# Perceiver block on one core: context loads placed between the transposes through DRAM, block-diagonal keys on ScalarE, the router's shares ahead of the softmax

## The chip, the core and the metric

The kernel runs on one core of a Trainium2 chip. The metric is the device time of one execution in microseconds (us). The kernel before was timed three times: 978.39 us median, 974.41 to 979.80. One execution was profiled; that one took 974.96 us, and its span, from the first to the last instruction in the trace, is 972.9 us. Engines in the profile: PE (TensorE matmuls), PEld (its weight loads), DVE (VectorE), ACT (ScalarE), POOL (GpSimd), SP (SyncE). ACTq, SPq and POOLq are the instruction queues of those engines where they issue DMAs.

## What is computed

There are 16 batches of 128 latent rows of 512 numbers, each with its own context of 2048 rows of 512, all float32. Per batch:

```python
x = x + softmax(LN(x) @ ctx.T) @ ctx          # cross attention, no scale, one head
h = LN(x)                                     # self attention, 16 heads of 32, causal
q, k, v = (h @ W_down) per head @ W_up        # half of q and k gets rotary positions
x = x + softmax(mask(q @ k.T / sqrt(32))) @ v @ Wc
h = LN(x)                                     # mixture of 8 experts of rank 64
gates = softmax over the top 2 of h[row 0] @ Wr.T
x = x + h + sum over the 2 of gate * (h @ A.T) @ B.T
```

Both experts are chosen for a whole batch by its first row.

## The kernel before, in words

The program is straight-line code for one core. A generator per batch and stage yields between small pieces of work, and `step(kind, batch, n)` runs the next n pieces. The order in which the pieces are issued is written out by hand: lines 616 to 668 for the start, the loop at line 671 for batches 0 to 13, lines 715 on for the last two. Matmuls, DMA issues and some others keep the order of the program on their engine; a scheduler may move the rest within an engine. Every engine then runs its own list strictly in order and waits on semaphores.

The stages of a batch, with the names that the profile shows:

- `score` (L250): normalizes x (`h_1`), turns it to `hT1`, multiplies it with the turned context `ctxT` in four parts v (`psc`, 32 matmul instructions each). ScalarE copies each to `sc` (L269), VectorE keeps a running maximum `mx`. Then the maximum over the context is spread over partitions (`tr_m`, `diag`, `spread`), added, and ScalarE takes the exponential (L297). A last piece adds up `sums` and `part` on VectorE.
- `attend` (L310): four parts of `av`, eight instructions each, and between the third and the last part `den`, the sum for the denominator, out of `part`. Then `x1` and its normalization `h_2`.
- `inner` (L332): `hT2`, then the projections `v`, `k` and `q` with folded weights. `rotated` (L360) applies the rotary positions: VectorE shuffles partners, GpSimd multiplies them (L376, `kP` and `qP`), VectorE multiplies and adds. `blocked` (L383) makes `kb`, k masked to one head of each pair, by four VectorE multiplies (L388). `compare` is `pss`, 16 instructions into four PSUM banks; `weigh` does the softmax of four heads at a time with VectorE and ScalarE (L415 to L429, 16 exps L424). Then `tr_p` transposes the probabilities on TensorE in four groups, ScalarE copies them out (`pT`, L167), and `y`, `o`, `x2` and `h_3` follow.
- `experts` (L563): `res = x2 + h_3` on GpSimd, `hT3`, `shares` (L472) and `route` (L487): `lg`, the logits, the two best, the indices, three gathers by indirect DMA on GpSimd's queue (`each` twice and `wb`), the copy `wa`, and the gate (L520 to L526). Then `mid`, `ffn`, the sum into `o` (L596) and its write to DRAM from GpSimd's queue (L597).

Batches overlap: while batch b is in `inner`, b+1 is in `attend`, b+2 in `score` and b-1 in `experts`. The pools p1, p2, p3, p4 hold one, two, three and four buffers of each name.

From batch 2 on (for hT1), from 1 to 14 (hT2) and from 0 to 13 (hT3), h is turned through DRAM: VectorE transposes blocks of 32x32 (`blocks`, L173), `send` (L142) writes them to a DRAM tile (`there`), and `fetch` (L150) reads them back in another order. Both are DMAs on SP's queue, and a fetch waits until its send has landed. In the loop the three transposes of a round are those of `3_{b-1}`, `2_{b+1}` and `1_{b+3}`.

The context goes through ScalarE's queue from the loop on: `load_ctx` and `load_turned` issue DMAs of 1 MB each, in ScalarE's program order, eight a batch. In the loop before, ctx 0, 1 and 2 of batch b+2 come between pieces of `inner` and `attend` (lines 683, 686, 690), and ctx 3 and the four ctxT of batch b+3 between the four `psc` of batch b+2 (lines 695 to 700), while `2_{b+1}` and then `1_{b+3}` are sent and fetched.

The few lines that place them, before:

```python
        step(inner, b + 1)
        send(f"2_{b + 1}")
        fetch(f"2_{b + 1}")
        step(experts, b - 1)
        for v in range(VC):
            step(score, b + 2)
            if v == 0:
                load_ctx(b + 2, [3])
            if b + 3 < B:
                load_turned(b + 3, [v])
```

Of the kernel before, what the change touches and what calls it, by code (L numbers as in the profile page):

```python
# [11 lines left out]
F32 = mybir.dt.float32  # L12
# [3 lines left out]
ALU = mybir.AluOpType  # L16
# [3 lines left out]
P = 128  # L20
# [48 lines left out]
def perceiver_block(ctx: ExitStack, tc: tile.TileContext, io: dict, out: bass.AP):  # L69
# [38 lines left out]
    def column(at):  # L108
        return cst[:, at : at + 1]
# [140 lines left out]
    def score(b):  # L250

        h = layernorm(xs[b], f"1_{b}", mix=b < 2)
        yield
        hT = p1.tile([P, 4, KC, QD], F32, tag="hT1", name=f"hT1_{b}")
        transposed(h, hT, f"1_{b}", b < 2)
        yield

        sc = p2.tile([P, VC, 4, S], F32, tag="sc", name=f"sc_{b}")
        mx = p1.tile([P, 4, S], F32, tag="mx", name=f"mx_{b}")
        for v, ct in enumerate(turned_cts.pop(b)):  # L260
            ps = bank(ps_sc, "sc", f"psc_{b}_{v}").rearrange("p (j t) -> p j t", j=4)
            for j in range(4):
                for c in range(KC):
                    matmul(
                        ps[:, j, :].rearrange("p (a i) -> p a i", a=4),
                        ct[:, c, j * P : (j + 1) * P], hT[:, :, c, :],
                        start=(c == 0), stop=(c == KC - 1),
                    )
            nc.scalar.copy(sc[:, v], ps)  # L269

            if v:
                nc.vector.tensor_tensor(mx, ps, mx if v > 1 else sc[:, 0], ALU.max)  # L272
            if v < VC - 1:
                yield

        def halved(t, op):
            nc.vector.tensor_tensor(t[:, :2], t[:, :2], t[:, 2:], op)
            nc.vector.tensor_tensor(t[:, 0], t[:, 0], t[:, 1], op)
            return t[:, 0]

        most = halved(mx, ALU.max)
        yield

        tr = bank(ps_tr, "tr", f"tr_m_{b}")
        transpose(tr[:, :S], most, ident)
        nm = p2.tile([P, 1], F32, tag="nm", name=f"nm_{b}")
        nc.vector.tensor_reduce(nm, tr[:, :S], AX.X, ALU.max, negate=True)
        diag = p1.tile([P, S], F32, tag="diag", name=f"diag_{b}")
        nc.vector.tensor_scalar(diag, ident, nm, None, ALU.mult)
        yield  # L290
        spread = bank(ps_tr, "tr", f"spread_{b}")
        matmul(spread[:, :S], ones, diag, start=True, stop=True)
        for v in range(VC):
            nc.vector.tensor_tensor(  # L294
                sc[:, v], sc[:, v], spread[:, None, :S].to_broadcast([P, 4, S]), ALU.add
            )
            nc.scalar.activation(sc[:, v], sc[:, v], AF.Exp)  # L297
        part = p2.tile([P, S], F32, tag="part", name=f"part_{b}")
        scores[b] = (sc, part)
        yield  # L300
        sums = p1.tile([P, 4, S], F32, tag="sums", name=f"sums_{b}")
        for v in range(1, VC):
            tc.keep_in_program_order(
                nc.vector.tensor_tensor(sums, sc[:, v], sums if v > 1 else sc[:, 0], ALU.add)
            )
        nc.vector.tensor_tensor(sums[:, :2], sums[:, :2], sums[:, 2:], ALU.add)
        nc.vector.tensor_tensor(part, sums[:, 0], sums[:, 1], ALU.add)
        yield

    def attend(b):  # L310

        sc, part = scores.pop(b)
        acc = bank(ps_acc, "acc", f"av_{b}")
        for v, ct in enumerate(cts.pop(b)):
            for j in range(4):
                matmul(
                    acc, sc[:, v, j, :], ct[:, j, :],
                    start=(v == 0 and j == 0), stop=(v == VC - 1 and j == 3),
                )
            if v == VC - 2:  # L320
                den = bank(ps_tr, "tr", f"den_{b}")
                matmul(den[:, :1], part, ones[:, :1], start=True, stop=True)
                rden = p2.tile([P, 1], F32, tag="rden", name=f"rden_{b}")
                nc.vector.reciprocal(rden, den[:, :1])
            if v < VC - 1:
                yield
        x1 = p2.tile([P, D], F32, tag="x1", name=f"x1_{b}")
        nc.vector.scalar_tensor_tensor(x1, acc, rden, xs.pop(b), ALU.mult, ALU.add)
        firsts[b] = (x1, layernorm(x1, f"2_{b}", mix=b in (0, B - 1)))
        yield  # L330

    def inner(b):  # L332
# [50 lines left out]
        def blocked():  # L383

            rotated("k", kT)
            for c in range(HC):
                kb = p4.tile([P, 2, S], F32, tag="kb", name=f"kb_{b}_{c}")
                nc.vector.tensor_tensor(  # L388
                    kb,
                    kT[:, c : c + 1, :].to_broadcast([P, 2, S]),  # L390
                    cst[:, C_BLK : C_BLK + 2, None].to_broadcast([P, 2, S]),
                    ALU.mult,
                )
                kbs.append(kb)

        def compare():

# [89 lines left out]
    def route(b, part):  # L487
# [29 lines left out]
            wa.rearrange("p c i r -> p i c r"), each.rearrange("p i (c r) -> p i c r", c=KC)  # L517
        )
        wa = wa.rearrange("p c i r -> p c (i r)")
        nm, ex, dn, gate = small(b, 1, "nm"), small(b, 1, "ex"), small(b, 1, "dn"), small(b, 1, "gate")  # L520
        nc.vector.tensor_scalar_mul(nm, top[:, 0:1], -1.0)
        nc.scalar.activation(ex, top[:, 1:2], AF.Exp, bias=nm)
# [6 lines left out]
    def early(b):  # L529
# [28 lines left out]
        part = shares(b, column_of(h, f"row_{b}"))  # L558
        yield
        route(b, part)  # L560
        yield

    def experts(b):  # L563

        x2, h = lasts.pop(b)
        res = p1.tile([P, D], F32, tag="res", name=f"res_{b}")
        if b < B - 2:
            nc.gpsimd.tensor_tensor(res, x2, h, ALU.add)
        else:
            nc.gpsimd.tensor_tensor(plain(res), plain(x2), mixed(h), ALU.add)  # L570
        hT = p1.tile([P, 4, KC, QD], F32, tag="hT3", name=f"hT3_{b}")
        transposed(h, hT, f"3_{b}", b >= B - 2)
        yield
        if b not in routes:
            part = shares(b, hT[:, 0, :, 0])
            yield
            route(b, part)
            yield
        wa, wb, gate = routes.pop(b)
        ps = bank(ps_acc, "acc", f"mid_{b}")  # L580
        for c in range(KC):
            matmul(
                ps[:, :S].rearrange("p (a i) -> p a i", a=4), wa[:, c, :], hT[:, :, c, :],
                start=(c == 0), stop=(c == KC - 1),
            )
        mid = p2.tile([P, S], F32, tag="mid", name=f"mid_{b}")
        nc.scalar.activation(mid, ps[:, :S], AF.Copy, scale=gate)
        yield
        o = p1.tile([P, D], F32, tag="o", name=f"out_{b}")

        n = D // 2 if b == B - 1 else D
        for at in range(0, D, n):
            cols = slice(at, at + n)
            ps = bank(ps_acc, "acc", f"ffn_{b}_{at}")
            matmul(ps[:, cols], mid, wb[:, cols], start=True, stop=True)
            nc.vector.tensor_tensor(o[:, cols], ps[:, cols], res[:, cols], ALU.add)  # L596
            (nc.sync if b == B - 1 else nc.gpsimd).dma_start(out[b][:, cols], o[:, cols])  # L597
        yield


# [66 lines left out]
    fold_turned(*ready)  # L667
    step(inner, 0)

    queue = nc.scalar  # L670
    for b in range(B - 2):
        if b + 3 < B:
# [2 lines left out]
        send(f"3_{b - 1}")  # L675
        fetch(f"3_{b - 1}")
        step(inner, b, 2)
        step(attend, b + 1)
        step(inner, b)
        step(score, b + 1)  # L680
        step(attend, b + 1)
        step(inner, b, 2)
        load_ctx(b + 2, [0])
        step(attend, b + 1)
        step(inner, b)
        load_ctx(b + 2, [1])
        step(experts, b - 1)
        step(attend, b + 1)
        step(inner, b)
        load_ctx(b + 2, [2])  # L690
        step(inner, b + 1)
        send(f"2_{b + 1}")
        fetch(f"2_{b + 1}")
        step(experts, b - 1)
        for v in range(VC):
            step(score, b + 2)
            if v == 0:
                load_ctx(b + 2, [3])
            if b + 3 < B:
                load_turned(b + 3, [v])  # L700
        step(inner, b)
        step(experts, b - 1)
        step(inner, b)
        step(experts, b - 1)
        step(inner, b)
        step(inner, b + 1)
        step(score, b + 2)
        step(score, b + 3, 2)
        send(f"1_{b + 3}")
        fetch(f"1_{b + 3}")  # L710
        step(inner, b)
        step(score, b + 2)

# [5 lines left out]
    step(inner, y, 2)  # L719
    step(attend, z)  # L720
    step(inner, y)
    step(score, z)
    step(attend, z)
    step(inner, y, 2)
    step(attend, z)
    step(inner, y)
    step(experts, y - 1)
    step(attend, z)
    step(inner, y)
    step(experts, y - 1)  # L730
# [10 lines left out]
    step(inner, z)  # L741
    step(experts, y)
    step(early, z)
    step(experts, y, 2)
    step(early, z)
    step(inner, z, 3)
    step(experts, y)
    step(inner, z)
    step(experts, y)
    step(experts, z, 3)  # L750


# [41 lines left out]
```

## Time and profile before

| | before |
|---|---|
| median of 3 runs | 978.39 us (974.41 to 979.80) |
| profiled execution | 974.96 us, span 972.9 us |
| PE busy | 863.3 us, 89% of the span |
| DVE, ACT, POOL busy | 511.7, 252.2, 169.6 us |
| DMA | 181.64 MB, 187 GB/s over the span |
| mean granted TensorE clock | 0.962 |
| loads of ctx and ctxT on ACTq | 56 and 52 DMAs of 1024 KB |
| sends and fetches on SPq | 42 and 42 of 256 KB |

How to read it. "X <- Y: total, times, longest" is a wait: instructions X stood idle, and the last thing they waited for was Y. A line of the chain of waits is start, length, what; it is the work that ended last, followed back. A line of the timeline is start, length, engine, source line, operation, out<-in, shapes, count, and in brackets the engine's idle time just before. L93 and L96 are the helpers that record every matmul and transpose, L101 the one that records DMA issues, so the tile's name tells the stage. A line of a table of stretches is from:to, length, busy time of PE, PEld, DVE, ACT and POOL with instruction counts, the granted clock, the busy share of the 16 DMA engines, and GB/s. Batch b's `pss` is the mark used for a period; in the trace those of batches 0, 1 and 14 start at 85.43, 137.77 and 891.45 us.

### The profile page before, as it was taken

What the parts mean: (1) busy time and instruction counts of PE and PEld (TensorE: products, weight loads), DVE (VectorE), ACT (ScalarE), POOL (GpSimd) and SP (SyncE); (2) the same over time, 40 slices, a digit from 0 to 9 for tenths busy, and PEclk for the clock granted to TensorE, in tenths of its full rate; (3) what the DMA queues carried; (4) which work ended last, traced back from release to release, by engine and by line L of the source; (5) the groups of instructions that cost most, each with busy time, mean ns of one, the idle gap of its engine ahead of it and who ended that gap; (6) DMA issues with size and microseconds to landing.
All of it is one profiled execution on the core that took longest, in us unless ns stands there. A gap on an engine that the chain in (4) does not pass through costs nothing.

```text
span 972.9 us, 14850 instructions
## 1 busy us (share of the span) xinstructions
PE 863.3 (89%) x5738; PEld 607.1 (62%) x5738; DVE 511.7 (53%) x1276; ACT 252.2 (26%) x787; POOL 169.6 (17%) x232
## 2 busy tenths in 40 slices
PE   7999998998979988899887989889799889999895
PEld 6846767565575755757555675655757557585653
DVE  1466374471835628275381744718356283837561
ACT  1232222231311322222222222313113222322340
POOL 1001012210122101212111121201221111121323
PEclk9999999998999999999899998999999999999987
DMA  9995819255282643808247182562826437240001
GB/s 362 347 407 198 311 44 355 99 213 222 81 313 84 253 181 149 306 23 344 100 162 281 31 348 98 189 244 82 311 85 259 174 152 292 85 166 22 22 18 58
DMA packets 57909, 181.64 MB, mean 187 GB/s; under 512 B 5504, under 2 KB 27392, under 8 KB 41456
## 3 DMA queue, kind: packets, MB, share of 16 engines
q10 hardware_dynamic: 15696, 113.32, 30.2%
q1 hardware_dynamic: 38064, 54.86, 15.6%
q0 software_dynamic: 4080, 12.53, 3.4%
q8 instruction: 45, 0.74, 0.3%
q14 instruction: 24, 0.20, 0.1%
HBM read 165.48 MB, written 15.20 MB: 186 GB/s over the span
## 4 chain that ended last, share of the span: by engine, by line
PE 47%; DMA 22%; DVE 18%; POOL 7%; issue 4%; ACT 2%; ACTq 0%; SPq 0%; POOLq 0%; DVEq 0%
PE av L93 17%; DMA hT<-there 15%; DMA there<-blocks 7%; PE o L93 6%; PE v L93 6%; PE psc L93 5%; DVE sc L294 3%; PE ffn L93 2%; DVE kb L388 2%; POOL rs L128 2%; DVE st L121 2%; POOL kP L376 2%; POOL qP L376 2%; PE y L93 2%; PE pss_sc L93 2%
## 5 line engine op out<-in xcount | busy, mean ns | idle before, releaser
L93 PE MATMUL psc<-hT,ctxT 128*128 128x128 f32 x2048 | 236.0, 278 | 1.4 <-ACT hT L167 1.4
L93 PEld LDWEIGHTS psc<-hT,ctxT 128*128 128x128 f32 x2048 | 233.3, 194 | 3.0 <-ACT hT L167 2.0
L93 PE MATMUL av<-ctx,sc 128*128 128x512 f32 x512 | 230.2, 598 | 0.0
L93 PEld LDWEIGHTS av<-ctx,sc 128*128 128x128 f32 x512 | 93.4, 190 | 104.3 <-issue 104.0
L424 ACT ACTIVATE att<-att,nmx 128x128 f32<-128x128 f32 x256 | 99.0, 388 | 196.0 <-DVE nmx L422 196.0
L125 POOL TENSOR_SCALAR rs<-mv 128x1 f32<-128x1 f32 x48 | 11.2, 233 | 461.3 <-DVE mv L123 445.9
L96 PE MATMUL tr_p<-ident,att 128*128 128x128 f32 x256 | 41.3, 306 | 46.7 <-ACT pT L167 46.7
L269 ACT COPY sc<-psc 128x512 f32<-128x512 f32 x64 | 37.5, 586 | 164.4 <-PE psc L93 164.4
L272 DVE TENSOR_TENSOR mx<-psc,mx 128x512 f32<-128x512 f32 x32 | 22.1, 691 | 91.9 <-ACT sc L269 91.9
L93 PE MATMUL v<-w_v,hT 128*32 128x512 f32 x512 | 61.1, 612 | 3.7 <-DMA hT<-there 2.8
L96 PEld LDWEIGHTS tr_p<-ident,att 128*128 128x128 f32 x256 | 33.0, 158 | 49.4 <-ACT pT L167 49.3
L297 ACT ACTIVATE sc<-sc 128x512 f32<-128x512 f32 x64 | 40.2, 630 | 90.9 <-DVE sc L294 90.4
L93 PE MATMUL o<-w_c,yT 128*128 128x512 f32 x128 | 60.9, 621 | 1.3 <-ACT yT L459 1.3
L93 PE MATMUL k<-hT,w_k 128*128 128x128 f32 x512 | 61.4, 279 | 0.7 <-ACT hT L167 0.7
L93 PEld LDWEIGHTS k<-hT,w_k 128*128 128x128 f32 x512 | 59.9, 196 | 1.8 <-ACT hT L167 0.9
L93 PE MATMUL q<-hT,w_q 128*128 128x128 f32 x512 | 59.8, 275 | 0.0
L93 PEld LDWEIGHTS q<-hT,w_q 128*128 128x128 f32 x512 | 58.5, 192 | 0.0
L596 DVE TENSOR_TENSOR out<-ffn,res 128x512 f32<-128x512 f32 (+1 forms) x17 | 11.2, 659 | 88.5 <-PE ffn L93 88.5
L167 ACT COPY pT<-tr_p 128x512 f32<-128x512 f32 x64 | 35.1, 592 | 68.8 <-DMA hT<-there 39.1
L424 ACT ACTIVATION_READ_ACCUMULATOR att<-att,nmx 128x1 f32 x256 | 47.7, 186 | 0.0
L294 DVE TENSOR_TENSOR sc<-sc,spread 128x512 f32<-128x512 f32 x64 | 42.6, 672 | 3.3 <-PE spread L93 3.3
L429 DVE TENSOR_TENSOR att<-att,rsm 128x512 f32<-128x512 f32 x64 | 43.6, 681 | 1.1
(127 smaller groups left out, 944.1 us busy)
## 6 DMA issues: line engine op xcount, KB each, us to landing
ctx<-in_ctx_dram ACTq DMA_DIRECT2D x56, 1024.0 KB
ctxT<-in_ctxT_dram ACTq DMA_DIRECT2D x52, 1024.0 KB
ctxT<-in_ctxT_dram SPq DMA_DIRECT2D x12, 1024.0 KB
there<-blocks SPq DMA_DIRECT2D x42, 256.0 KB
hT<-there SPq DMA_DIRECT2D x42, 256.0 KB
ctx<-in_ctx_dram SPq DMA_DIRECT2D x8, 1024.0 KB
x<-in_x_dram SPq DMA_DIRECT2D x16, 256.0 KB
out_dram<-out POOLq DMA_DIRECT2D x15, 256.0 KB, 2.9
```

Source lines behind the costliest of these rows:

```text
L93: tc.keep_in_program_order(nc.tensor.matmul(*args, **kwargs))
L96: tc.keep_in_program_order(nc.tensor.transpose(*args))
L121: nc.vector.bn_stats(stats, src)
L128: nc.gpsimd.tensor_tensor(rstd, rstd, mhalf[:n], ALU.pow)
L167: nc.scalar.copy(dst[:, :, first : first + 4, :].rearrange("p a n j -> p n a j"), tr.rearrange("p (n a j) -> p n a j", n=4, a=4),)
L269: nc.scalar.copy(sc[:, v], ps)
L272: nc.vector.tensor_tensor(mx, ps, mx if v > 1 else sc[:, 0], ALU.max)
L294: nc.vector.tensor_tensor(sc[:, v], sc[:, v], spread[:, None, :S].to_broadcast([P, 4, S]), ALU.add)
L297: nc.scalar.activation(sc[:, v], sc[:, v], AF.Exp)
L376: nc.gpsimd.tensor_tensor(partner, partner, cst[:, None, C_SIN : C_SIN + S].to_broadcast([P, HC, S]), ALU.mult)
L424: nc.scalar.activation(att[:, i, :], att[:, i, :], AF.Exp, bias=nmx[:, i : i + 1], scale=SCALE, accum_out=sm[:, i : i + 1],)
L429: nc.vector.tensor_tensor(att[:, hs, :], att[:, hs, :], rsm[:, hs, None].to_broadcast([P, 4, S]), ALU.mult)
```

## The change

- hT1 gets two buffers instead of one.
- `den` moves behind the last part of `av` for batches 1 to 14.
- `kb` is one tile made by two ScalarE activations (copy with a per-partition scale) instead of four tiles by four VectorE multiplies.
- `route` ends with the gathers; the gate's part is a function of its own, `gates`, issued in a later piece.
- `experts` adds `ffn` into `res` and writes `res` to DRAM; the tile `o` is gone.
- The loop is reordered: `experts` of b-1 takes its shares and `route` between pieces of `inner` and `attend`, that is ahead of the softmax; the sums of `score` come later; the four ctx loads of b+2 stand together behind the third `psc`, after the sends of `2_{b+1}` and `1_{b+3}`; ctxT 0 and 1 of b+3 come once `inner` of b+1 has issued its v, and ctxT 2 and 3 of b+2 at the start of the next round, behind the fetch of `3_{b-1}`.
- In the tail, `o` of batch 15 stands ahead of `mid` of batch 14.

```diff
-        hT = p1.tile([P, 4, KC, QD], F32, tag="hT1", name=f"hT1_{b}")
+        hT = p2.tile([P, 4, KC, QD], F32, tag="hT1", name=f"hT1_{b}")
...
-            if v == VC - 2:
+            if v == (VC - 1 if 0 < b < B - 1 else VC - 2):
                 den = bank(ps_tr, "tr", f"den_{b}")
...
-            for c in range(HC):
-                kb = p4.tile([P, 2, S], F32, tag="kb", name=f"kb_{b}_{c}")
-                nc.vector.tensor_tensor(
-                    kb,
-                    kT[:, c : c + 1, :].to_broadcast([P, 2, S]),
-                    cst[:, C_BLK : C_BLK + 2, None].to_broadcast([P, 2, S]),
-                    ALU.mult,
-                )
-                kbs.append(kb)
+            kb = p1.tile([P, HC, 2, S], F32, tag="kb", name=f"kb_{b}")
+            for half in range(2):
+                nc.scalar.activation(
+                    kb[:, :, half, :], kT, AF.Copy, scale=column(C_BLK + half)
+                )
+            kbs.extend(kb[:, c] for c in range(HC))
...
+        routes[b] = (wa, wb, top)
+
+    def gates(b):
+        wa, wb, top = routes[b]
         nm, ex, dn, gate = small(b, 1, "nm"), small(b, 1, "ex"), small(b, 1, "dn"), small(b, 1, "gate")
...
             route(b, part)
             yield
+            gates(b)
+            yield
...
-            nc.vector.tensor_tensor(o[:, cols], ps[:, cols], res[:, cols], ALU.add)
-            (nc.sync if b == B - 1 else nc.gpsimd).dma_start(out[b][:, cols], o[:, cols])
+            nc.vector.tensor_tensor(res[:, cols], ps[:, cols], res[:, cols], ALU.add)
+            (nc.sync if b == B - 1 else nc.gpsimd).dma_start(out[b][:, cols], res[:, cols])
...
         step(inner, b, 2)
+        if b:
+            load_turned(b + 2, [2, 3])
         step(attend, b + 1)
         step(inner, b)
+        step(experts, b - 1)
+        step(attend, b + 1)
+        step(experts, b - 1)
+        step(inner, b, 2)
         step(score, b + 1)
         step(attend, b + 1)
-        step(inner, b, 2)
-        load_ctx(b + 2, [0])
+        step(inner, b)
         step(attend, b + 1)
         step(inner, b)
-        load_ctx(b + 2, [1])
         step(experts, b - 1)
-        step(attend, b + 1)
-        step(inner, b)
-        load_ctx(b + 2, [2])
         step(inner, b + 1)
         send(f"2_{b + 1}")
         fetch(f"2_{b + 1}")
-        step(experts, b - 1)
-        for v in range(VC):
-            step(score, b + 2)
-            if v == 0:
-                load_ctx(b + 2, [3])
-            if b + 3 < B:
-                load_turned(b + 3, [v])
+        step(score, b + 3, 2)
+        send(f"1_{b + 3}")
+        step(score, b + 2, 3)
+        load_ctx(b + 2)
+        step(score, b + 2)
+        fetch(f"1_{b + 3}")
         step(inner, b)
...
         step(inner, b + 1)
+        if b + 3 < B:
+            load_turned(b + 3, [0, 1])
         step(score, b + 2)
-        step(score, b + 3, 2)
-        send(f"1_{b + 3}")
-        fetch(f"1_{b + 3}")
         step(inner, b)
         step(score, b + 2)
...
     step(early, z)
+    step(experts, y, 3)
+    step(early, z)
+    step(inner, z, 4)
     step(experts, y, 2)
-    step(early, z)
-    step(inner, z, 3)
-    step(experts, y)
-    step(inner, z)
-    step(experts, y)
     step(experts, z, 3)
```

## The prediction

> **What bounds the kernel now.** I read TensorE's waits first, then the chain of waits, then the timeline around the largest wait, and last a table of stretches.
>
> TensorE's waits (us in total, times, longest):
> ```profile
> PE tr_p L96 <- ACT pT L167: 46.7, 11, 5.0
> PE pss_sc L93 <- DVE qT L379: 22.9, 15, 1.6
> PE lg L93 <- DVE g_part L484: 13.1, 14, 1.0
> ```
> Three waits recur, the first in 11 batches, the others in nearly all; the rest are single ones. The first says that ScalarE's copy of pT came late. The chain of one period (start, us, what) says why:
> ```profile
> 507.49 2.23 DMA there<-blocks
> 509.81 15.47 DMA hT<-there
> 525.30 0.33 ACTq L101
> 525.73 0.59 ACT pT L167
> 526.37 1.11 PE tr_p L96 x4
> ```
> A transpose through DRAM is open for 17.7 us, of which 15.47 are its second half. Then ScalarE's queue issues a load (ACTq L101), and only then copies pT. The order of the built program names the link: the load of ctxT v=3 waits on the semaphore that hT2's fetch raises, because DMAs share a few semaphores in turn, and pT's copies stand behind it. The timeline shows the same instant:
> ```profile
> 519.19 0.59 ACT L269 COPY sc<-psc 128x512 f32<-128x512 f32 x1 [2.99 <-PE psc L93]
> 525.30 0.33 ACTq L101 DMA_DIRECT2D ctxT<-in_ctxT_dram  x1
> 525.73 1.07 ACT L167 COPY pT<-tr_p 128x512 f32<-128x512 f32 x2 [5.95 <-DMA hT<-there]
> 526.37 1.11 PE L96 MATMUL tr_p<-ident,att 128*128 128x128 f32 x4 [5.01 <-ACT pT L167]
> 527.28 1.93 PE L93 MATMUL ffn<-wb,mid 128*128 128x512 f32 x2
> ```
> ScalarE stands from 519.8 to 525.7, TensorE 5.01 us, and after it runs at half speed for a while: ffn takes 1.93, against 1.02 where nothing stalled (at 816.69). Why the fetch takes 15.47 is seen by its twin at 545.08, which has no loads beside it. In the stretches its bytes stand alone (DMA share, GB/s last):
> ```profile
> 546.00:548.00 2.00, 2.00 (x6) 0.76 (x4) 2.00 (x7) 0.00 (x0) 0.00 (x0) 1.00 0.43 131
> 548.00:550.00 2.00, 0.43 (x1) 0.00 (x0) 1.13 (x3) 0.00 (x0) 1.27 (x1) 1.00 0.00 0
> 512.00:518.00 6.00, 6.00 (x57) 6.00 (x56) 1.38 (x2) 1.17 (x2) 1.48 (x2) 1.00 1.02 413
> ```
> All its data moved before 548, under 3 us after issue; at 512 to 518 the same fetch shares full DMA engines with context loads.
>
> What a period costs, from the start of one batch's pss to the next (columns: length, PE busy, ..., clock, DMA):
> ```profile
> 490.72:550.05 59.33, 51.76 (x345) 36.50 (x346) 31.41 (x80) 15.09 (x48) 10.42 (x14) 0.97 0.49 187
> 838.95:891.45 52.50, 49.94 (x345) 35.82 (x346) 29.87 (x76) 15.13 (x48) 9.63 (x12) 1.00 0.33 116
> ```
> The second period is the last of the loop, with no further context to load: same matmuls, no pT wait, 52.50 us, clock 1.00. From batch 1's pss (137.77) to batch 14's (891.45) the 13 periods average 57.98. TensorE bounds it, with stalls of about 8 us a period.
>
> **The change, part by part.** t is time from a period's pss; durations are those of the rows above and of the timeline.
>
> *Loads.* ctxT 2 and 3 are issued behind the new kb on ScalarE (t about -1.6), ctx 0 to 3 behind the copy of psc 2 (t 24.1), ctxT 0 and 1 behind vv (t 36). In the built program none of them waits for a transpose still open: their semaphores belong to DMAs that landed over 5 us earlier. So ScalarE no longer stands before pT, and the 5.01 us with the slow matmuls go. The bounds of this term are nothing (a load still finds a wait of its own) and 5.01 plus the slow clock; I take the whole, because the period without the wait stands in the trace. What is late next: v needs hT2. den ends at t 12.8; behind it VectorE still has two multiplies, six small operations and 1/den, so x1 ends near 14.8; statistics, GpSimd's rstd (0.8), two normalizations and the block transpose bring blocks to 19.5; there lands 2.2 later, the clean fetch 2.9 after that, at 24.6. v starts at 31.6 (psc ends at 27.2, then tr_p, mid, tr_p, ffn and y, 4.4): 7 us to spare. hT1 follows by t 25.3, while the first load's data start near 25.5. Eight issues of 0.33 to 0.45 us stand on ScalarE beside psc and o, under 1.7 us together between two psc copies 3.6 apart: hidden. At the start SP issued five such loads from 1.18 to 4.05 us without standing, so four in a row should pass; if the cover were gone the delay would be that 1.7. The 6.3 MB of ctx and ctxT 0, 1 at the 404 GB/s seen at 26 to 36 us take 15.6 us, to t 41; hT3's fetch is issued at t 45. Context is first needed at t 46 (ctx) and t 62.8 (psc).
>
> *kb on ScalarE.* Four VectorE multiplies (1.37 us in the chain at 545.78) become two ScalarE operations of 128x512. No row has that operation; a plain copy of this size takes 0.59, an exp 0.63, and mid, with the same kind of scale on 128x128, 0.37: between 0.4 and 0.63 each. I take 0.6, the rows of its size, so 1.2 together, started when kT is ready (t -3.4) on an idle ScalarE: done at -2.1, ahead of pss. qT's chain (shuffle 0.7, GpSimd 1.27, add 0.69) starts 1.37 earlier and ends at av's end, so of the 1.62 wait about 0.1 is left. GpSimd's two products are then the end of it.
>
> *Shares and route.* g_share now runs right after qT, ahead of the softmax, and lg stands between av 1 and av 2. hT3 lands at t -2.2, g_share wants it at -0.1, lg at 5.4: the 0.94 wait goes. The softmax's sums move behind route's small operations, and den behind the last av. The VectorE walk, with the steps of batch 15's rows (922.36 on) and starting at its gap of 1.16: two adds and two reduces of 0.61 to 3.55, then two maxima, two adds and two reduces to 6.15 (ScalarE's exps run from 3.8, 1.55 a group of four), the first multiply to 6.75, lg's copy, a reciprocal, maxima for the third group (7.2), top, the second multiply to 7.95, the index, the first sum to 8.7, maxima for the fourth group (8.9; its exps end at 10.6), two more sums with blocks, row and rows between them to 10.75, the half sum to 11.1, two reciprocals, part at 11.6. den wants it at 12.64 (1.92 pss, 3.49 av, 0.25 lg, 6.98 two av). Zero cost, 1.0 spare; the bounds are that and the 2 us of rival 1. lg's own place costs TensorE the same 0.25 as before.
>
> *Others.* hT1 with two buffers and res instead of o remove or add waits that rows show as long over; g_ex is issued before psc, hidden behind 16 exps.
>
> Sum of a period: 52.50 - 1.62 - 0.94 + 0.1 = **50.05**, and the busy column of that period, 49.94, agrees. 13 x (57.98 - 50.05) = 103.1.
>
> *First period* (85.43 to 137.77, 52.34): it has a wait of 2.33 for hT2 (at 118.03) and 1.5 for qT: -3.8.
>
> *Tail* (891.45 to 972.90). For batch 15 den stays before the last av, but its part now comes at 11.7 while den's turn is 9.15: +2.6, bounds +1.5 to +6 (the upper with the last av's 3.5 us at half speed). h_2 loses its queue of g_ operations: -0.3. The o projection of batch 15 (953.45) stands ahead of mid_14, which waited for GpSimd's wa: yT can be copied at 950.2, so o starts 3.25 earlier, and GpSimd's rstd no longer stands behind the result's write (0.6): about -4.5 at the last add, where res_15 waits for res_14's write to land (2.9) and comes in just beside ffn. Together -2.2, bounds -4 to +2.
> Whether the 2.6 us cool the clock: after 2.33 idle v still took 3.64, full speed; after 2.48 and 0.68 idle k took 5.27 against 3.74. I take no cooling. The Trainium skill (TensorE: Matmul & The Clock Gate, Part 1) has the clock halved only after an idle window of about 3.4 us; by it this is safe too, by k's row the tail is 1.5 longer.
>
> Total: 972.9 - 103.1 - 3.8 - 2.2 = 863.8, plus the 2.06 around the span (974.96 - 972.9) = 865.9. The profiled execution lies 0.35% under the median 978.39; scaled by it: **869**.
>
> **Rivals.**
> 1. *A new wait per period.* The margin of den (1.0) is worked from steps of 0.1 to 0.7, and qT and av end within 0.2 of each other. If two of them cost 1 to 2 us a period: 13 to 26 more, 882 to 895. For: the walk is long. Against: every step has a row. 0.16.
> 2. *The result's write holds res.* res has one buffer, and GpSimd's res, ahead of the product for kP, waits until the last write has landed. Issue t 31.7, res wanted at 41.9. Rows have the write at 2.4 to 4.5; if it stretched to 15.5 beside the loads as the fetch did, res ends 3.4 us after kP's turn: 13 x 3.4 = 44, 913. Against: its rows are 2 KB, the fetch's 512 B. 0.05. The Trainium skill (DMA: Bandwidth & Descriptors, Queues, rings and completion order) has each DMA engine take turns between queues packet by packet; by that a write in a quarter of the packets should stretch to about 4 us, an estimate, and res stays free.
> 3. *Slower: hT3's fetch meets loads.* g_share stands ahead of the whole softmax. If ctx and ctxT 0, 1 run past t 45, that is under 6.3 MB / 19.5 us = 323 GB/s, the fetch takes 15.5, lands at 10.5, and the softmax starts 9.7 late: lg stalls 5.4, den 3.3, slow clock 1.5: period 60.2, 13 x 2.2 = 29 over before, less 6 elsewhere: 1001. Against: full engines show 391 to 423 GB/s everywhere. 0.05.
> 4. *It doesn't separate them*: the pT wait stays, only 2.5 a period go: 978 - 13 x 2.5 - 6 = 940. Against: the waits in the built program. 0.03.
>
> **Numbers.** Forecast 0.71, rivals 0.16, 0.05, 0.05, 0.03. Faster (a measurement tells 0.5% from no change) 0.93, within 0.5% 0.02, slower 0.05. The range takes the forecast's tail bounds and rival 1: 861 to 895.
>
> **What would show it.** Right: the wait of tr_p on pT is gone from TensorE's list, periods of 50 us from pss to pss, fetches under 4 us, DMA busy in blocks only between hT1's landing and the next there. Wrong: g_share waiting for hT3, den for part, res for the write, or ACTq loads in the chain; each names its rival. A batch 15 den wait near 2.6 tests the tail.

## The result, and the profile after

The kernel after takes 866.01 us (median of 4 runs, 862.40 to 875.42), against 976.40 for the kernel before in the same comparison (971.68 to 979.80): a ratio of 0.886, 95% interval 0.880 to 0.892. The run of 875.42 is a slow one and is not in the ratio. The prediction was 869 us, in a range of 861 to 895. The profiled execution took 863.91 us, its span is 862.1 (before 972.9), its mean granted TensorE clock 0.993 (before 0.962).

TensorE is busy for 829.9 us, 96% of the span (before 863.3, 89%). Three of its waits in the kernel after (us in total, times, longest):

```profile
PE pss_sc L93 <- DVE g_share L473: 7.0, 14, 0.8
PE den L93 <- DVE part L307: 1.9, 1, 1.9
PE lg L93 <- DVE g_part L481: 1.0, 1, 1.0
```

The 46.7 us of tr_p behind pT are gone from the list. lg's 13.1 became a single wait of 1.0, and pss's 22.9 became 7.0. One period in the table of stretches:

```profile
583.92:634.08 50.16, 49.67 (x345) 36.07 (x346) 29.58 (x75) 16.48 (x50) 10.99 (x14) 1.00 0.60 222
```

A period is 50.16 us with TensorE busy for 49.67 of them at full clock, where the period of the kernel before that the prediction shows had 59.33 with 51.76 at 0.97. The timeline of the same period shows the new order around the transposes:

```profile
580.19 0.37 SPq L101 DMA_DIRECT2D hT<-there  x1
580.86 0.72 ACT L388 ACTIVATE kb<-kT,cst 128x512 f32<-128x512 f32 x1 [2.79 <-DVE kT L379]
580.91 0.82 ACTq L101 DMA_DIRECT2D ctxT<-in_ctxT_dram  x2
583.92 1.14 PE L93 MATMUL pss_sc<-kb,qT 64*128 64x256 f32 x8 [0.47 <-DVE g_share L473]
...
605.04 0.37 SPq L101 DMA_DIRECT2D hT<-there  x1
607.62 2.00 ACTq L101 DMA_DIRECT2D ctx<-in_ctx_dram  x4
608.63 0.37 SPq L101 DMA_DIRECT2D hT<-there  x1
```

hT3's fetch (580.19) leaves 0.72 us ahead of two ctxT loads, hT2's (605.04) 2.6 us ahead of four ctx loads. Both landed in 2.8 to 2.9 us. hT1's (608.63) leaves 1.0 us behind the first of those four, and took 14.5 us: one of the three transposes still meets the loads. Nobody needs it before the next round's psc. The DMA list has the medians of all fetches and of the result's writes:

```profile
hT<-there SPq DMA_DIRECT2D x42, 256.0 KB, 2.9
out_dram<-res POOLq DMA_DIRECT2D x15, 256.0 KB, 6.6
```

Term by term, in spans of the two profiled executions:

| term | predicted | measured |
|---|---|---|
| start, to batch 0's pss | 0 | 83.55 - 85.43 = -1.9 |
| first period | -3.8 | 48.66 - 52.34 = -3.7 |
| 13 periods | 13 x (50.05 - 57.98) = -103.1 | 784.55 - 132.21 = 652.3, 50.18 each: -101.3 |
| tail | -2.2 | 77.55 - 81.45 = -3.9 |
| span | 863.8 | 862.1 |

The periods gained 1.8 us less than the sum had, the start and the tail 3.6 more: that the span came within 1.7 us is in part errors that cancel.

### The profile page after: what moved, and what is told of

The parts are those of the page before. It is cut to its first block, busy times and chain, and to the rows that moved or that the text cites. A ratio compares the mean times of both kernels' runs of the same rounds, so it can differ in the third digit from the quotient of the medians.

```text
span 862.1 us, 14782 instructions
## 1 busy us (share of the span) xinstructions
PE 829.9 (96%) x5738; PEld 597.5 (69%) x5738; DVE 482.9 (56%) x1212; ACT 274.3 (32%) x819; POOL 177.4 (21%) x232
## 4 chain that ended last, share of the span: by engine, by line
PE 72%; DVE 11%; DMA 7%; POOL 6%; issue 2%; ACT 1%; ACTq 0%; POOLq 0%; DVEq 0%
PE psc L93 27%; PE av L93 20%; DMA ctxT<-in_ctxT_dram 7%; PE v L93 6%; PE o L93 3%; PE tr_p L96 3%; PE pss_sc L93 2%; POOL kP L376 2%; POOL qP L376 2%; DVE sc L294 2%; PE y L93 2%; PE mid L93 2%; PE ffn L93 2%; PE pss_acc L93 2%; DVE qP L371 1%
## 5 line engine op out<-in xcount | busy, mean ns | idle before, releaser
L503 POOL DMA_INDIRECT each<-in_A_dram,g_blocks x32 | 37.9, 1186 | 159.4 <-DVE g_row L499 154.4
L93 PE MATMUL v<-w_v,hT 128*32 128x512 f32 x512 | 58.9, 592 | 0.9 <-DVE w_v L219 0.9
L600 POOL DMA_DIRECT2D out_dram<-res x15 | 10.0, 665 | 189.2 <-DVE res L599 189.2
L131 DVE TENSOR_SCALAR h<-x,mv,rs 128x512 f32<-128x512 f32 x48 | 27.5, 573 | 32.0 <-POOL rs L128 32.0
L93 PEld LDWEIGHTS o<-w_c,yT 128*128 128x128 f32 x128 | 24.4, 201 | 25.1 <-issue 24.1
```

The source lines that it names most:

```text
L93: tc.keep_in_program_order(nc.tensor.matmul(*args, **kwargs))
L131: nc.vector.tensor_scalar(to, of, mv[:, 0:1], rstd, ALU.subtract, ALU.mult)
L503: nc.gpsimd.indirect_dma_start(each[:, i, :], None, io["A"], bass.IndirectOffsetOnAxis(ap=blocks[:, i : i + 1], axis=0),)
```

## The experiments

The theory: before lost time in two ways that the loads' place caused together. (a) A link: ScalarE stood at the load of ctxT v=3, which waits for hT2's fetch, with pT's copies queued behind it. (That the wait goes by a shared semaphore was read from the built program; a trace shows only when the load leaves.) (b) Contention: that fetch took 15 us beside loads and 2.9 alone. kb on ScalarE takes pss's wait, and the shares ahead of the softmax take lg's. Rivals: contention alone; link alone; or a gain from the third part (shares, den, gates, res, order of the experts).

### The three parts, alone and together

The third part is the rest of the change. The order in which hT1 is sent and fetched moves with the loads and with the third part alike, so it is new in every cell but "neither" and "kb" of the old place; hT1's second buffer is in all cells of the new place and, of the old place, in "both". A cell is the ratio to the kernel before on the same chip, its 95% interval, and the median; before took 978.07, 980.57 and 977.32 us in the three comparisons of this section, and 976.40 in the change's own.

| | loads at the old place | loads at the new place |
|---|---|---|
| neither | 1 | 0.901 (0.896 to 0.906), 881.14 |
| kb on ScalarE | 0.978 (0.972 to 0.984), 955.06 | 0.885 (0.880 to 0.889), 863.76 |
| third part | 0.980 (0.974 to 0.986), 958.31 | 0.922 (0.915 to 0.930), 903.47 |
| both | 0.982 (0.976 to 0.988), 961.07 | 0.886 (0.880 to 0.892), 866.01 |

**The loads' place alone** (b_loads): before, with hT1 in two buffers and, in the loop,

```diff
+        if b:
+            load_turned(b + 2, [2, 3])
         step(attend, b + 1)
...
-        load_ctx(b + 2, [0])
...
-        for v in range(VC):
-            step(score, b + 2)
-            if v == 0:
-                load_ctx(b + 2, [3])
-            if b + 3 < B:
-                load_turned(b + 3, [v])
+        step(score, b + 3, 2)
+        send(f"1_{b + 3}")
+        step(score, b + 2, 3)
+        load_ctx(b + 2)
+        step(score, b + 2)
+        fetch(f"1_{b + 3}")
...
         step(inner, b + 1)
+        if b + 3 < B:
+            load_turned(b + 3, [0, 1])
         step(score, b + 2)
-        step(score, b + 3, 2)
-        send(f"1_{b + 3}")
-        fetch(f"1_{b + 3}")
```

> The kernel before with the loads alone placed as in the change (and hT1 with two buffers, which their place needs); kb on VectorE, shares and den as before. Theory 1 (the place of the loads is the bulk): the wait of tr_p on pT goes, those of pss (1.6) and lg (0.94) stay, the period falls from 57.98 to 52.5, the first period loses its 2.3: 976.4 - 71 - 2.3 = about 902. Theory 2 (the shorter chains on VectorE made the gain, the loads only move the wait): about 960 or more, with a wait of ScalarE or of v for hT2 in place of the old one.

It measured 881.14 us, 21 less than the theory expected: periods of 51.30 (pss at 133.43 to 800.30). The wait of tr_p on pT is gone and pss's is as before (22.8 us in 15 waits). Most of the surplus is lg's wait: in 14 batches before, it is a single one of 0.9 us here, without the shares being moved, and 13 x 0.94 is 12 us. The start gives 1.8 and the tail 2.4 more; the rest was not followed up. VectorE's timeline before, and then in this kernel, has the order that the scheduler chose:

```profile
503.47 0.75 DVE L328 SCALAR_TENSOR_TENSOR x<-av,rden,x 128x512 f32<-128x512 f32 x1 [1.32 <-PE av L93]
504.14 0.18 DVE L484 TENSOR_REDUCE g_part<-g_share 128x8 f32<-128x32 f32 x1
```
```profile
555.34 0.18 DVE L484 TENSOR_REDUCE g_part<-g_share 128x8 f32<-128x32 f32 x1
...
556.57 0.74 DVE L328 SCALAR_TENSOR_TENSOR x<-av,rden,x 128x512 f32<-128x512 f32 x1
```

Before, g_part stood behind x1, which waited 1.32 us for av. With the new loop it stands ahead of it. The edit moves hT1's transpose as well as the loads; that the loads alone matter is seen below in `a_old_loads`, which keeps hT1's new order and buffer and puts only the loads back.

**kb alone** (b_kb): before, with the change's hunk for `kb` and nothing else.

```diff
-            for c in range(HC):
-                kb = p4.tile([P, 2, S], F32, tag="kb", name=f"kb_{b}_{c}")
...
+            kb = p1.tile([P, HC, 2, S], F32, tag="kb", name=f"kb_{b}")
+            for half in range(2):
```

> The kernel before with kb alone moved to ScalarE. Theory 1: qT's chain is on the path in every period, whatever follows: pss's wait falls from 1.62 to the 0.47 that the changed kernel shows, 14 x 1.15 = 16 less, about 960. Theory 2: the slow fetch sets the period from one batch to the next and swallows it: 976, with pT's wait longer by 1.15.

The time is as expected, but not for the expected reason alone. The largest of TensorE's waits in this kernel:

```profile
PE v L93 <- DMA hT<-there: 56.7, 13, 5.6
```

pss's wait shrank from 22.9 to 6.6, and lg's is a single one of 0.9 here too. tr_p no longer waits at all: in the period from 481.80 the load of ctxT v=3 leaves at 509.41, long before hT2's fetch (508.72, 9.1 us) has landed. (In the built program it waits for an earlier ctx load; why this edit deals the semaphores out otherwise, no run shows.) The wait for hT2 comes up at v instead, a few microseconds later. It is not the fetch alone: hT2's write to DRAM (499.78) leaves 1.05 us behind a ctxT load and takes 8.9 us, where in the kernel before it left 1.04 ahead of the next load and took 2.23. So (a) can go by accident, and (b) then costs nearly as much by itself.

**Loads and kb, without the third part** (b_loads_kb): the two edits above together.

> Loads and kb together, in the kernel before. If the parts add: 902 - 16 = about 886, period 51.35; the remaining 20 to the changed kernel's 866 are then lg's wait (0.94 x 13 = 12), the tail (4) and the start. If one hides the other: 902.

863.76 us, periods of 50.15: all of the change's gain. It is 22 us below the sum of the parts, because the loads alone were already 21 below theirs. What the third part adds is 866.01 against 863.76, with intervals that overlap (0.880 to 0.889 and 0.880 to 0.892): nothing that these runs can tell.

**The third part and kb, without the loads' place** (a_old_loads): the kernel after, with the loads at before's lines, between pieces of `attend` and `inner`, and

```diff
-        step(score, b + 2, 3)
-        load_ctx(b + 2)
-        step(score, b + 2)
+        for v in range(VC):
+            step(score, b + 2)
+            if v == 0:
+                load_ctx(b + 2, [3])
+            if b + 3 < B:
+                load_turned(b + 3, [v])
```

> The changed kernel with the loads alone put back to where they stood before. In its built program no load in front of pT's copies waits for a fetch (the semaphores fall out differently), so ScalarE does not stand; but the fetch of hT2 meets 4 to 5 MB of loads again. Theory 1b (contention costs by itself): hT2 lands 13 to 15.5 us after its issue at 21 us into the period, v's turn is at 31.6: v waits 3 to 5 us, with a slower clock behind it up to 6.5: 905 to 950. Theory 1a alone (only ScalarE's standing costs): 866.

961.07, more than expected: as long as v waits, this is no better than kb alone.

```profile
PE v L93 <- DMA hT<-there: 57.0, 13, 5.9
```

The link is not quite gone either, as the expectation had it. In the 13 rounds with ctxT loads one of them leaves less than 0.1 us ahead of hT2's fetch, that is when hT2's write has landed (511.80 and 511.83 in the period from 482.94), and ScalarE stands until then. It costs tr_p little, 3.6 us in 6 waits. And the third part quite alone (b_shares), the same kernel with hT1 in one buffer and kb by VectorE's four multiplies:

> The kernel before with the third part alone: the shares ahead of the softmax, den behind the last transpose, the gates later, the result added in place, the new order of the experts' steps; loads, hT1's buffer and kb as before. Theory 'this part is worth nothing': the 5 us waits at pT or at hT2's v stay, 970 to 985 us; lg's wait of 0.9 us may go, 14 times, without a gain larger than 13 us. Rival 'it is worth lg's wait': 962 to 966 us.

958.31, below both expectations. tr_p's wait has gone here too, and v waits for hT2 50.6 us in 13 waits: one took the other's place. lg's wait is a single one of 1.0, and those 12 us are most of the 14.7 by which the span is shorter. So lg's wait is what the third part has to give here; kb alone, or the loads' place alone, takes it as well, and with either of them there is nothing left for the third part.

### Link or contention

**One load moved** (b_last_late): before, with only ctxT v=3 issued behind vv's copy, so that no copy of pT stands behind it:

```diff
-            if b + 3 < B:
+            if b + 3 < B and v < VC - 1:
                 load_turned(b + 3, [v])
...
         step(inner, b + 1)
+        if b + 3 < B:
+            load_turned(b + 3, [VC - 1])
```

> The kernel before with one load, ctxT v=3, moved from before pT's copies to behind vv's copy on ScalarE; all other loads stay, so the transposes are as slow as before. Theory 1a (the stall came by ScalarE standing at that load until hT2's fetch had landed): ScalarE no longer stands, tr_p's wait goes, the fetch still takes 15 us and v waits for it some 1.5 us: period about 54, 13 x 4 = 52 less, about 924. Theory 1b (the slow fetch itself is what bounds the period): the same time passes at v in place of tr_p: about 975.

918.26 us, ratio 0.940 (0.934 to 0.946), periods of 53.9, and no wait of tr_p. What is left of (b) is v's wait:

```profile
PE v L93 <- DMA hT<-there: 15.6, 12, 2.2
```

The moved load did not make the fetch shorter: in the period from 458.65 it takes 16.18 us and lands at t 35.2, in the kernel before, in the period from 490.72, at t 34.6. But v starts at t 35.4 here and at 39.6 there. So the link is confirmed, at some 4 us a period. The kernel before holds a control of its own, the last period with all eight loads:

```profile
785.78:838.95 53.17, 50.15 (x346) 35.95 (x346) 31.42 (x80) 15.13 (x48) 10.43 (x14) 1.00 0.53 203
```

There the load of ctxT v=3 left at 814.31 and pT did not wait; hT2's fetch left at 804.87, among the loads, and v started at 819.17 after 0.45 us of waiting. (In four of before's eleven waits the trace names hT1's write and not hT2's fetch; in the period from 137.77 that write landed at 170.83, after the load had left at 170.56, so it did not hold the load.)

**The ctx loads two pieces earlier** (a_ctx_early): the kernel after with the four ctx loads behind the first psc:

```diff
-        step(score, b + 2, 3)
-        load_ctx(b + 2)
         step(score, b + 2)
+        load_ctx(b + 2)
+        step(score, b + 2, 3)
```

> The changed kernel with the four ctx loads two psc parts earlier, behind the copy of psc 0 (17 us into the period in place of 24), so that they run beside hT2's send and fetch (issued at 19 and 21). If the fetch takes its 15.5 us whenever loads run: it lands at 36.7, v (31.6) waits 5 and runs slow behind it: 13 x 6 = 78 more, about 944. If it is slow only as long as loads are in flight (4.2 MB at 0.4 MB per us, 18.5 to 29): it lands at about 31, and the 7 us of spare time hide it: 866 to 875.

873.37, ratio 0.891 (0.886 to 0.895), an interval that overlaps after's: v waits 4.6 us in 8 waits, up to 1.5. In the period from 486.77 hT2's write takes 7.3 us and the fetch 6.6, landing at t 32.8, near the 31 of the second expectation and not at 36.7. So a transpose is slow only for as long as loads are under way with it. ScalarE stood at the ctx loads here (56.5 us in 12 waits of a copy of psc), and TensorE did not wait for it: standing costs only where something that is needed stands behind.

### The third part's price: who holds the ctxT loads back

**kb on VectorE again** (a_kb_dve), in the kernel after: before's four multiplies in place of the two activations.

> The changed kernel with kb back on VectorE, in four multiplies. If qT's chain is on the path: pss's wait goes from 0.47 back to 1.6, 13 to 14 x 1.15 = 15 to 16 more, about 881. If VectorE has room there: 866.

903.47: 37 us more. Beside pss's 22.9 us, den waits 14.7 in 11 waits. The timeline shows why:

```profile
445.92 0.82 ACTq L101 DMA_DIRECT2D ctxT<-in_ctxT_dram  x2
446.65 0.37 SPq L101 DMA_DIRECT2D hT<-there  x1
...
454.28 0.21 DVE L476 TENSOR_TENSOR g_share<-w_r,hT 128x32 f32<-128x32 f32 x1 [2.82 <-DMA hT<-there]
```

Without kb's activations, which wait for kT, ScalarE issues the two ctxT loads 0.7 us ahead of hT3's fetch instead of 0.7 behind it. The fetch takes 7.6 us, the shares wait for it ahead of the softmax, and den waits for what stands behind. This is rival 3's mechanism, with other loads: rival 3 had those of ctx and ctxT 0 and 1 run late, here ctxT 2 and 3 leave early.

**The same, with these two loads behind the first two groups of the softmax** (a_kb_dve_late):

```diff
-        if b:
-            load_turned(b + 2, [2, 3])
         step(attend, b + 1)
...
         step(inner, b, 2)
+        if b:
+            load_turned(b + 2, [2, 3])
```

> The kernel after with kb made by VectorE (a_kb_dve, 903.5 us), and the ctxT loads for pieces 2 and 3 issued behind the first two groups of the softmax on ScalarE instead of ahead of them. Theory 'kb on ScalarE also holds these two loads back until the fetch of hT3 is through': the load leaves ScalarE only when the exponentials have, hT's fetch lands in about 3 us again, den's wait (2.5 us, 11 times) is gone and only the longer pss wait stays (1.6 against 0.5 us, 14 times, 15 us): 878 to 886 us. Rival 'VectorE's own six block operations push the shares and the softmax back': den's wait stays and the time is 898 to 906 us.

886.38 (883.64 to 887.09), ratio 0.908 (0.903 to 0.913), just above the first theory's 878 to 886. den's wait is one of 1.9 in the last batch, periods are 51.33 on average, and the timeline has the fetch by itself, 2.8 us long:

```profile
486.99 0.37 SPq L101 DMA_DIRECT2D hT<-there  x1
...
491.82 0.20 DVE L476 TENSOR_TENSOR g_share<-w_r,hT 128x32 f32<-128x32 f32 x1
...
496.67 0.34 ACTq L101 DMA_DIRECT2D ctxT<-in_ctxT_dram  x1
```

So kb on ScalarE does two things in the change: it takes 1.15 us out of pss's wait, and it is the gate that holds two loads until the fetch has left. With kb on VectorE the gate is worth the 17 us between 903.47 and 886.38.

**Rival 3 forced** (a_ctxT_first): the kernel after with all four ctxT loads ahead of hT3's fetch, and the two other places empty.

```diff
+        if b:
+            load_turned(b + 2)
         step(experts, b - 1)
         send(f"3_{b - 1}")
```

> The changed kernel with the four ctxT loads of a round issued together behind the exponentials of sc, ahead of kb, just as hT3 is sent and fetched (the third rival of the prediction, made to happen). 4.2 MB run from 4 us before pss to 6 us after it. If hT3's fetch is slowed, it lands about 7 us into the period, g_share and with it the whole softmax wait, lg stalls some 2 us and den some 2.7: 13 x 4.6 = 60 more, about 926. If the softmax has room for it: 866.

955.82, ratio 0.977 (0.971 to 0.982). lg waits 39.2 us in 14 waits, up to 3.8, and den 22.3 in 12, up to 3.1, as rival 3 described. The price is half again what was expected. These waits are 61.5 us, 58.6 more than in the kernel after, and the span is 92.5 longer; the mean clock is 0.965 against 0.993, which over 954.6 us is some 27 more, an estimate.

### Two versions that try for pss's last half microsecond

**After, with k's rotation ahead of the transpose for the experts** (a_den_k), and den of the last batch behind its last av:

```diff
-            if v == (VC - 1 if 0 < b < B - 1 else VC - 2):
+            if v == (VC - 1 if 0 < b else VC - 2):
...
+        step(inner, b)
         step(experts, b - 1)
         send(f"3_{b - 1}")
         fetch(f"3_{b - 1}")
-        step(inner, b, 2)
+        step(inner, b)
```

> The kernel after with k's rotation of a batch ahead of the transpose of the batch before's expert input, and den of the last batch behind its last transpose. Theory 'pss waits 0.47 us because ScalarE's block copies start when VectorE is done with kT, and VectorE can be done earlier by the norm's transpose copies': pss's wait goes (14 x 0.47 = 6.6 us) and den's last wait of 1.9 us too: 857 to 860 us. Rival 'the fetch of hT3 then starts about 1.3 us later, and the shares wait for it': pss's gain is given back at den or lg, 864 to 880 us.

929.63, ratio 0.951 (0.946 to 0.956): 64 us slower than the change. pss's wait did go (one of 0.6 us and one of 0.5 are left), but two queues have changed places:

```profile
458.31 0.82 ACTq L101 DMA_DIRECT2D ctxT<-in_ctxT_dram  x2
459.35 0.37 SPq L101 DMA_DIRECT2D hT<-there  x1
467.97 0.21 DVE L473 TENSOR_TENSOR g_share<-w_r,hT 128x32 f32<-128x32 f32 x1 [6.80 <-DMA hT<-there]
478.32 0.38 PE L93 MATMUL den<-ones,part 128*128 128x1 f32 x2 [2.51 <-DVE part L307]
```

pss stands at 461.39 here. kb starts 3.1 us ahead of it, as in the kernel after; the fetch leaves 2.0 ahead, not 3.7. So the loads now leave 1.04 us ahead of the fetch, and it takes 8.6 us. The rival had the delay of the fetch (1.3 expected) and the waits of lg and den that follow (11.3 and 32.6 us in all); that the fetch would fall behind the loads neither theory saw. By these rows that is 5.8 us (8.6 against 2.8) of the 6.8 that g_share waits. The mean clock of 0.966 adds some 25 us by the same estimate as above; the span is 65.8 longer than after's.

**Loads, kb and the same edit of the loop, without the third part** (b_loads_kb_k):

> The kernel before with the loads' new place and kb on ScalarE (863.8 us), and k's rotation ahead of the transpose of the expert input. By the first theory of a_den_k pss's wait of 0.47 us goes 14 times: 857 us. By its rival the shares stand late in VectorE's order here, so a later fetch does not show: also 857. Where both kernels gain nothing, kT is not what pss waits for: 864 us.

859.95 (857.59 to 861.83), ratio 0.881 (0.878 to 0.885), the lowest of all, with an interval that overlaps those of the change and of `b_loads_kb`. The fetch leaves 1.05 us behind the loads here too, but the shares stand late on VectorE, and nothing waits:

```profile
574.58 0.82 ACTq L101 DMA_DIRECT2D ctxT<-in_ctxT_dram  x2
575.63 0.37 SPq L101 DMA_DIRECT2D hT<-there  x1
...
588.62 0.21 DVE L473 TENSOR_TENSOR g_share<-w_r,hT 128x32 f32<-128x32 f32 x1
```

Its stretch from 578 to 627, nearly one period of 49.61, has TensorE busy throughout at full clock; what is left is TensorE's own work:

```profile
578.00:627.00 49.00, 49.00 (x345) 35.58 (x341) 29.47 (x76) 16.41 (x50) 10.55 (x14) 1.00 0.60 220
```

## Why the prediction came out

- **Loads.** The mechanism held in both halves, link and contention. The price was taken from before's last period, and that period was misread: it was said to have no further context to load. The DMA list of 838.95 to 891.45 has four loads, half of the usual eight:

```profile
ctx<-in_ctx_dram ACTq DMA_DIRECT2D x4, 1024.0 KB
```

  The price was right even so, because TensorE waited there for qT and g_part alone, that is neither for pT nor for hT2. v did not wait in the change, as its 7 us of spare time said. One step failed without a price: hT1's fetch was to land by t 25.3, ahead of the loads' data; it landed at about t 39 (608.63 + 14.5 - 583.92), since the first of the four loads leave before it does. Four issues in a row held ScalarE for 2.00 us, where 1.7 was allowed.
- **kb.** 0.72 and 0.71 us in place of 0.6 each. pss keeps 0.47 of its wait instead of 0.1, 14 times. The trace puts it to g_share, which starts when qT is done; `b_loads_kb` has no g_share there and waits as long (6.6 us in 14), for qT. The term is small, but a second effect was not in the sum: the activations gate two loads. The change gained by this gate without the prediction having seen it, which was luck: the same reasoning for a kernel with kb on VectorE would have missed 17 us.
- **Shares.** The period's sum took 0.94 for lg's wait and gave it to the shares. The time did go, and `b_shares` shows that the shares can take it; but the loads' place alone and kb alone take it too, so in this change the step has the right size and the shares add nothing. den's margin was worked out as 1.0; in the trace part ends at t 11.1 and den stands at 12.56. The walk along VectorE was good to half a microsecond.
- **Rival 1** did not come in the change; den waited in three versions where hT3's fetch left behind loads, 1.3 (14.7 / 11) to 2.5 us (32.6 / 13) a time; it did not in `b_loads_kb_k`, where the shares stand late. **Rival 2** came by half: the write stretched to 6.6 us (longest 8.0) and res had 10 us. By the Trainium skill (DMA: Bandwidth & Descriptors, Queues, rings and completion order) I had put it at about 4, an estimate that was too low; a stretch smaller than the fetch's (14.5 us) it did have right. **Rival 3** was nearer than its chance said. I argued it from the loads' rate; what decides is which of two instructions, 0.7 us apart on two queues, leaves first. **Rival 4** did not come.
- **Start** was costed at nothing. hT1's second buffer lets batch 1's score run on at the start (a wait of 0.73 us on hT at 26.89 before is gone): batch 0's pss comes at 82.2 to 83.6 us in the ten kernels with it, and at 84.1 to 85.4 in the four without.
- **Tail.** den of the last batch waited 1.86 us, against 2.6 predicted; the av behind it ran at full speed (8 matmuls in 3.68 us), so no cooling, as assumed. k took 3.84 instead of 5.27 and batch 15's o 3.70 instead of 5.16: the tail ran warmer than the sum had it. These are 2.9 us, more than the 1.7 by which the term was short; what took the rest back was not followed up.

## What to carry to other kernels

Before you price a reordering of loads, find a stretch of the same trace in which the waits in question do not come up: it gives the size of link and contention together, which pricing either alone would miss. Then read from the DMA list of that stretch what else is different in it. For a short transfer beside long loads, look at which instruction leaves first, not only at which bytes overlap, and write down what holds the later one back, because a harmless edit upstream can take that away. Moving a consumer earlier gains little when another edit takes its wait away as well, and it makes the kernel depend on every transfer that feeds it.

## What the runs showed of the hardware that was not expected

**A short transfer's length depends on who leaves first.** The same fetch of 256 KB took 2.8 us when issued 0.72 us ahead of two 1 MB loads, 7.6 when 0.73 behind them, 8.6 when 1.04 behind, and 14.5 when 1.0 behind the first of four. It is so in nearly every round: hT3's fetch, 0.56 to 0.80 us ahead of the two loads, took 2.5 to 3.0 us in the ten rounds of the kernel after that were read, and 0.73 to 2.63 us behind them it took 7.3 to 8.6 in 22 rounds of `a_kb_dve` and `a_den_k`, with no order by the distance. hT1's fetch, 0.66 to 2.19 us behind the first of four loads, took 13.5 to 16.1 us in nine rounds of the kernel after, and 6.2 and 8.7 in two. The write of 256 KB took 2.23 us when 1.04 ahead of a load, and 8.9 when 1.05 behind one.

**A wait of 2.5 us can halve the clock, and later than the wait.** After den's wait of 2.51 in the version with k ahead, the stretches show the clock (the column behind POOL's):

```profile
478.60:478.80 0.20, 0.20 (x3) 0.20 (x4) 0.20 (x2) 0.00 (x0) 0.07 (x1) 1.00 0.00 0
478.80:479.00 0.20, 0.20 (x3) 0.20 (x3) 0.20 (x2) 0.00 (x0) 0.20 (x1) 0.53 0.00 0
...
482.20:482.50 0.30, 0.30 (x4) 0.30 (x4) 0.30 (x1) 0.00 (x0) 0.00 (x0) 0.95 0.79 314
```

TensorE works again from 478.32. It runs at full clock until 478.81 (0.53 over 0.2 us is full for 0.01 and half for the rest), at half until 482.23 (0.95 over 0.3), 3.4 us in all. The Trainium skill (TensorE: Matmul & The Clock Gate, Part 1) has windows of about 3.4 us, and an idle one halves the clock; the length agrees with these rows. But the 3.4 us ahead of the drop were not all idle: TensorE worked for about 0.9 of them, to 475.8 and from 478.32. The length of a wait alone does not decide. The clock fell after 2.51 us here, after 2.19 ahead of v in `b_last_late` (v took 5.34 us), and after 2.48 with 0.68 behind it in the kernel before (k took 5.27). It did not fall after den's 1.86 us in the kernel after, nor after these two waits of 2.67 and 0.67 us:

```profile
803.17 0.66 PE L96 MATMUL tr<-ident,h 128*128 128x128 f32 x4 [2.67 <-DVE h L131]
804.50 3.84 PE L93 MATMUL k<-hT,w_k 128*128 128x128 f32 x32 [0.67 <-ACT hT L167]
```

That it is the place of the wait in such a window that decides would fit these rows; no run here shows it.
